# Attention: the second projection of a tile is issued behind the weighing product

## The chip, the cores and the metric

The kernel runs on one core of a Trainium2 chip. The metric is the device time of one execution in microseconds; the figure of merit is the median of repeated runs. Five engines of the core work side by side, each on its own list of instructions in order: TensorE (PE) multiplies matrices and transposes, ScalarE (ACT) applies functions and copies, VectorE (DVE) and GpSimd (POOL) work elementwise, SyncE (SP) issues transfers. They wait for each other through semaphores. In the profile PEld stands for the weight loads of TensorE.

## The reference, cut to what matters

Four layers run one after the other on a batch of four images of 64x64 pixels with 128 channels. The first three (two state-space scans and an edge-weighted mixing layer) take over nine tenths of the time and are not touched. The change lies in the fourth, neighbourhood attention with four heads of 32 channels, where each pixel looks at a 7x7 window around itself:

```python
qkv = (x @ qkv_w + qkv_b).reshape(B, H, W, 3, HEADS, HEAD_DIM)
q = qkv[..., 0, :, :] * HEAD_DIM ** (-0.5)
kk = qkv[..., 1, :, :]
v = qkv[..., 2, :, :]
...
scores = jnp.einsum('bxyhd,bxyklhd->bxyhkl', q, kwin) + bias[None]
attn = jax.nn.softmax(scores.reshape(B, H, W, HEADS, k * k), axis=-1)
...
out = jnp.einsum('bxyhkl,bxyklhd->bxyhd', attn, vwin).reshape(B, H, W, C)
return out @ proj_w + proj_b
...
gate = jax.nn.sigmoid(jax.nn.relu(x @ g1_w + g1_b) @ g2_w + g2_b)
return attn_out * gate + x
```

## The kernel before, in words

The class `Attention` (from L1964) works on tiles of 128 queries, that is two image rows; 32 tiles make an image (`NQ`), 128 tiles the batch. For a tile the keys are eight image rows, that is 512 pixels or one matmul of 512 columns for each head; a bias with a large negative number outside the 7x7 window does the masking. One tile passes through these steps, each a small method:

- `scores` (L2102, PE): four heads, 128x512 scores into a PSUM tile of four banks, `sps`, of which there is one.
- `biased` (L2113, DVE), one call for each head: adds the bias, negates and takes the minimum.
- `exponential` (L2126, ACT), one call for each head, with the row sum.
- `turn` (L2134, PE), one call for each head: four 128x128 transposes into a PSUM bank of the tag `tps`; `keep` (L2141) copies the bank to SBUF, heads 0 and 1 on ACT, heads 2 and 3 on DVE.
- `one_over` (L2155 on DVE, L2157 on POOL): the reciprocal of the row sums, spread to 128 columns.
- `weigh` (L2151, PE): the weighing product, values times turned weights, all heads, into one quarter of the PSUM tile `d`.
- `turn_others` (L2162, L2163, PE): transposes of the reciprocals and of x, into two other quarters of `d`; `inverse` (L2167, ACT) copies the first of them out.
- `divide` (L2171, DVE), then `mix` (L2174, PE: the output projection), then `result` (L2180, L2181, DVE) and the store of the result by SP (L2184).

The steps of several tiles are interleaved: a pass of the loop in `run` over `n` issues the scores of tile n, turns tile n-1, weighs tile n-2 and finishes tile n-3. The order of the calls in the loop is the order of each engine's list; the layer runs under a manual schedule, so nothing rearranges it.

Into the same loop go the projections. `project(b, c)` returns small functions, the pieces, for one chunk c of 512 pixels (four tiles), two chunks ahead of its use (`LEAD`):

- query and key: one fp32 matmul of 512 columns (L2045, L2051) and an ACT instruction that adds the bias (L2047, L2052);
- hidden: the same with 64 outputs (L2056, L2058);
- values: four matmuls of 128 columns (L2075) and one ACT copy (L2080);
- gates: four matmuls of one column (L2063), one ACT instruction (L2067) and two short DVE instructions (L2068, L2069).

A chunk has these five pieces, and the chunks 0 and 7 of an image a second values piece at the end. They are dealt to the four passes of a group:

```python
left = 4 - n % 4
now, pieces = pieces[: -(-len(pieces) // left)], pieces[-(-len(pieces) // left) :]
```

Five pieces thus fall as query+key, hidden, values, gates; six as query+key, hidden+values, gates, values. Below, a pass is called by its pieces: the query-key pass, the hidden pass and so on. Thirty chunks are projected inside the loop (two before it), so there are 30 query-key passes, and of these chunks seven have six pieces and so a hidden-values pass too: 37 passes with two pieces.

Every turn and every piece takes one bank of the tag `tps`, and there are two of them. A turn or a piece can therefore start only when the bank taken two steps earlier has been read out: by the copy of `keep`, or by the ACT instruction of the piece. In a query-key pass the banks are taken in the order turn of head 3 (tile n-2), query, key, turns of heads 0, 1, 2 (tile n-1).

Of the kernel before, what the change touches and what calls it, by code (L numbers as in the profile page):

```python
# [1870 lines left out]
def layer2(tc, C, nb, x_in, x_out, d_w, d_rel, d_v, beside, side):  # L1871
    with ExitStack() as es, tc.manual_schedule():
# [12 lines left out]
        if True:  # L1885
            with tc.tile_pool(name="last", bufs=1) as pool:
                E.pool = pool
                last = Last(tc, C, pool, E.psum, side, nb - 1, x_in)
                last.early()
                run(statistics(0, range(NCH)))  # L1890
                last.late()
                E.roots([E.rstd])
                for _ in in_turn([last.first(c) for c in range(NCH)]):
                    pass
                pieces = project(0, range(4))
                for _ in in_turn([last.second(c) for c in range(NCH)]):
                    for _ in range(2):
                        if pieces:
                            pieces.pop(0)()
                run(pieces)  # L1900
# [31 lines left out]
            gates, gather = E.gates(out, last[2], [third[2]["var"]], []), E.gather(*last, alone=True)  # L1932
            pieces = E.finish(*third)
            run(gates[:1] + rest[:2] + gates[1:2] + rest[2:4] + gates[2:4] + rest[4:] + pieces[:4] + gates[4:6])
            run(pieces[4:] + gather[:3] + E.outputs(*second) + gather[3:])
            E.roots([second[2]["var"]])
# [27 lines left out]
class Attention:  # L1964
# [221 lines left out]
    def run(self):  # L2186

        nc, total = self.nc, self.nb * NQ

        def do(f, n, *args):  # L2190
            if 0 <= n < total:
                f(n, *args)

        def chunk_of(m):
            return divmod(m, NCH)

        for m in range(self.LEAD):
            for piece in self.project(*chunk_of(m)):
                piece()
            self.load(*chunk_of(m + 2))  # L2200
            if m == 0:
                for i in range(3):
                    self.bring_bias(i)
        pieces = []
        for n in range(total + 4):
            if n % 4 == 0 and n < total:
                assert not pieces
                m = n // 4 + self.LEAD
                self.load(*chunk_of(m + 2))
                if m < self.nb * NCH:  # L2210
                    pieces = self.project(*chunk_of(m))
                if n in (4, 8):
                    self.bring_bias(2 + n // 4)
            left = 4 - n % 4
            now, pieces = pieces[: -(-len(pieces) // left)], pieces[-(-len(pieces) // left) :]
            do(self.scores, n)
            do(self.turn, n - 2, 3)
            do(self.biased, n, 0)
            do(self.biased, n, 1)
            do(self.one_over, n - 1)  # L2220
            do(self.keep, n - 2, 3, nc.vector.tensor_copy)
            do(self.exponential, n, 0)
            do(self.exponential, n, 1)
            for piece in now:
                piece()
            do(self.biased, n, 2)
            do(self.biased, n, 3)
            do(self.mix, n - 3)
            do(self.turn, n - 1, 0)
            do(self.turn, n - 1, 1)  # L2230
            do(self.keep, n - 1, 0, nc.scalar.copy)
            do(self.exponential, n, 2)
            do(self.keep, n - 1, 1, nc.scalar.copy)
            do(self.result, n - 3)
            do(self.weigh, n - 2)
            do(self.turn_others, n - 2)
            do(self.exponential, n, 3)
            do(self.inverse, n - 2)
            do(self.divide, n - 2)
            do(self.turn, n - 1, 2)  # L2240
            do(self.keep, n - 1, 2, nc.vector.tensor_copy)
# [211 lines left out]
```

## Time and profile before

| | |
|---|---|
| median of three runs | 13013.98 us (13012.62 to 13024.42) |
| the profiled execution's own time | 13014.66 us |
| its span, first to last instruction | 13012.9 us |
| busy share of the span | DVE 90%, POOL 74%, PE 72%, ACT 60% |
| scores of tile 0, of tile 127 | at 12140.0 us, at 12995.5 us of the span |

The shares are means over four layers. The attention lies in the last 870 us, and only its own part of the profile bears on the change. Times in the rows below are microseconds from the span's start; "x4" counts instructions merged into a row; what stands in brackets at the end of a row is the time that the engine stood idle before it, and the instruction that ended this. The ends of PE's rows are modelled, the starts are recorded.

### The profile page before, as it was taken

Reading aid. Unit: us, or ns where it says so; the run is one execution under the profiler, and the core shown is the slowest. Engines: PE = TensorE matmul, PEld = TensorE weight load, DVE = VectorE, ACT = ScalarE, POOL = GpSimd, SP = SyncE. Lnnn points to the kernel's source line nnn. Section 1 sums busy time; section 2 is a strip of 40 time slices with the busy share of each in tenths; the row PEclk is TensorE's granted clock in tenths of the full one; section 3 lists DMA queues with packets and bytes.
Section 4 is the critical chain, followed back from the end, with each engine's and each line's share of the span. In section 5 each row is a group of like instructions: output and inputs, shape, how many; then the busy total and the mean of one; then the engine's idle time right before and its main releaser. Section 6 shows DMA issues by size and latency. Waiting matters only on the chain.

```text
span 13012.9 us, 128062 instructions
## 1 busy us (share of the span) xinstructions
PE 9421.2 (72%) x40881; PEld 2750.7 (21%) x41435; DVE 11773.1 (90%) x7219; ACT 7773.2 (60%) x10392; POOL 9663.5 (74%) x3167
## 2 busy tenths in 40 slices
PE   6777677677777767777777677777777776765799
PEld 1111111111111111111111111112111121211455
DVE  8999999999999889999999899999999998587566
ACT  4666566665666556655666565555555554575576
POOL 6887888887878778887888788888888887165200
PEclk8888999889988888988988898888899898987899
DMA  6888888898888978898878887777887776144300
GB/s 181 211 226 229 221 221 218 216 232 216 211 224 206 219 196 212 219 227 215 211 215 214 225 209 195 206 202 198 216 202 197 199 202 175 52 121 122 72 21 18
DMA packets 873450, 2463.66 MB, mean 189 GB/s; under 512 B 141888, under 2 KB 163528, under 8 KB 865096
## 3 DMA queue, kind: packets, MB, share of 16 engines
q1 hardware_dynamic: 872775, 2455.44, 73.5%
q8 instruction: 330, 5.41, 0.2%
q14 instruction: 345, 2.82, 0.1%
HBM read 2035.79 MB, written 268.17 MB: 177 GB/s over the span
## 4 chain that ended last, share of the span: by engine, by line
DVE 34%; issue 18%; PE 15%; DMA 15%; POOL 9%; ACT 8%; SPq 2%; DVEq 0%; another core or an unknown queue 0%; POOLq 0%; ACTq 0%
DVE h L478 18%; DVE h L459 12%; DMA h<-dud 7%; POOL h L459 5%; PE ms L102 3%; PE da L467 2%; POOL delta L102 2%; ACT da L469 2%; PE yps L559 1%; ACT s L2126 1%; DMA repC<-xdd 1%; POOL low L102 1%; DVE s L2113 1%; PE B L504 1%; DMA pad<-xid 1%
## 5 line engine op out<-in xcount | busy, mean ns | idle before, releaser
L459 POOL TENSOR_TENSOR h<-h,repC 128x2048 f32<-128x2048 f32 x1536 | 6956.0, 4534 | 1488.1 <-ACT state L496 1196.8
L478 DVE TENSOR_TENSOR_SCAN h<-da,state,h 128x1024 f32<-128x1024 f32 x2304 | 5294.1, 2338 | 277.7 <-ACT da L469 164.7
L469 ACT ACTIVATE da<-da,av 128x1024 f32<-128x1024 f32 x3072 | 3327.7, 1087 | 2895.3 <-PE da L467 2463.6
L467 PE MATMUL da<-dp,spread 128*128 128x512 bf16 x5802 | 2007.3, 426 | 2409.5 <-DVE h L478 2373.2
L459 DVE TENSOR_TENSOR h<-h,B 128x2048 f32<-128x2048 f32 x1536 | 3476.8, 2264 | 184.0 <-issue 78.9
L559 PE MATMUL yps<-h,gather 128*32 128x512 f32 x12288 | 1878.5, 687 | 18.0 <-issue 5.9
L478 DVE TENSOR_TENSOR_SCAN h<-da,h 128x1024 f32<-128x1024 f32 x768 | 1719.6, 2278 | 73.7 <-ACT da L469 35.2
L467 PEld LDWEIGHTS <-spread 128*128 128x128 bf16 x6144 | 589.9, 102 | 4479.2 <-issue 4091.8
L565 PE MATMUL yps<-ones,nothing 128*128 128x512 bf16 x4197 | 1243.6, 406 | 38.5 <-issue 34.9
L102 ACT ACT_TABLE_LOAD x580 | 744.1, 1283 | 12.6 <-DMA x<-in_x_dram 2.4
L102 ACT CAST parts<-delta 128x1024 bf16<-128x1024 f32 x384 | 400.7, 1043 | 565.0 <-POOL delta L102 539.1
L565 PEld LDWEIGHTS <-nothing 128*128 128x128 bf16 x4409 | 384.9, 101 | 1234.2 <-issue 945.4
L102 POOL TENSOR_TENSOR delta<-delta,low 128x1024 f32<-128x1024 f32 x192 | 452.0, 2354 | 258.0 <-ACT low L102 206.6
L2157 POOL COPY wide_total<-total 128x128 f32<-128x128 f32 x128 | 37.8, 296 | 780.6 <-DVE total L2155 214.3
L102 PE MATMUL ms<-d,wts 128*128 128x512 f32 (+3 forms) x832 | 481.9, 691 | 165.1 <-POOL d L102 59.8
L102 PE MATMUL ms<-xd,xpdt 64*128 64x512 f32 x768 | 481.9, 710 | 105.3 <-ACT xd L102 24.5
L102 POOL TENSOR_TENSOR low<-delta,xc 128x1024 f32<-128x1024 f32 x192 | 502.9, 2619 | 9.1
L2126 ACT ACTIVATE s<-s,least 128x512 f32<-128x512 f32 x512 | 368.5, 720 | 230.1 <-DVE least L2113 224.5
L542 PE MATMUL yps<-y,ident 128*128 128x512 f32 x576 | 497.4, 953 | 4.4 <-issue 1.3
L102 ACT ACTIVATE low<-ms,av 128x512 f32<-128x512 f32 x384 | 263.9, 687 | 291.1 <-PE ms L102 264.9
L1792 POOL TENSOR_TENSOR acc<-acc,part 128x1024 f32<-128x1024 f32 x120 | 303.8, 2535 | 174.7 <-DVE part L1786 174.7
L102 POOL TENSOR_TENSOR parts<-delta,parts 128x1024 bf16<-128x1024 f32 x192 | 409.6, 2134 | 31.8 <-ACT parts L102 28.8
(295 smaller groups left out, 11071.5 us busy)
## 6 DMA issues: line engine op xcount, KB each, us to landing
h<-dud SPq DMA_DIRECT2D x3072, 512.0 KB
dp<-parts SPq DMA_DIRECT2D x2304, 64.0 KB
repC<-xdd SPq DMA_DIRECT2D x192, 512.0 KB
dud<-low SPq DMA_DIRECT2D x192, 512.0 KB
spread<-gd SPq DMA_DIRECT2D x72, 1024.0 KB
pad<-xid SPq DMA_DIRECT2D x176, 256.0 KB
x<-x SPq DMA_DIRECT2D x104, 256.0 KB
yd<-y SPq DMA_DIRECT2D x96, 256.0 KB
```

What stands on the lines that cost most here:

```text
L102: return call(*args, **kw)
L459: engine.tensor_mul(pair, pair, t.prepared[step][name].unsqueeze(1).to_broadcast([P, 2, TS]))
L467: self.nc.tensor.matmul(da[:, cols], self.C.spread[:, jj, :], dp[:, j, cols], start=True, stop=True)
L469: self.nc.scalar.activation(da, da, AF.Exp, scale=t.W.a[:, at : at + 1])
L478: nc.vector.tensor_tensor_scan(h[:, way], da[:, way], h[:, way], 0.0 if step % NSTEP == 0 else t.states[step - 1][:, u % NG : u % NG + 1], ...
L504: self.nc.tensor.matmul(rep[:, self.half(i)], t.W.pick[at, :], t.prepared[step]["xd"][at, :], start=True, stop=True)
L542: self.nc.tensor.matmul(self.like_part(yps, k), self.C.ident, self.part(t.y, k, c, b), start=True, stop=False)
L559: self.nc.tensor.matmul(out, self.C.gather[jj], rhs, start=False, stop=jj == 3)
L565: self.nc.tensor.matmul(self.live["yps"], self.C.nothing, self.C.ones16, start=False, stop=False, skip_group_check=True)
L1792: (nc.vector if alone and pair else nc.gpsimd).tensor_add(acc, acc, part)
L2113: self.nc.vector.tensor_tensor_reduce(out=self.live["s", n][:, h, :], in0=self.live["sps", n][:, h, :], in1=self.bias[case][:, h, :], scal ...
L2126: self.nc.scalar.activation(s, s, AF.Exp, scale=-1.0, bias=self.live["least", n][:, h : h + 1], accum_out=self.live["total", n][:, h : h + 1],
```

## The change

In each pass, only the first of the pass's pieces stays at its place, ahead of the last two `biased`. The second, where there is one, is issued after `weigh(n - 2)` and ahead of `turn_others(n - 2)`. In a query-key pass this moves the key, in a hidden-values pass the values. On PE the piece passes from ahead of `mix`, two turns and the weighing product to behind them; on ACT from ahead of `keep` of head 0, `exponential` of head 2 and `keep` of head 1 to behind them, still ahead of `exponential` of head 3 and `inverse`. The banks are then taken in the order turn of head 3, first piece, turn 0, turn 1, second piece, turn 2. Instructions and data stay the same.

```diff
             do(self.exponential, n, 0)
             do(self.exponential, n, 1)
-            for piece in now:
+            for piece in now[:1]:
                 piece()
             do(self.biased, n, 2)
             do(self.biased, n, 3)
...
             do(self.keep, n - 1, 1, nc.scalar.copy)
             do(self.result, n - 3)
             do(self.weigh, n - 2)
+            for piece in now[1:]:
+                piece()
             do(self.turn_others, n - 2)
             do(self.exponential, n, 3)
             do(self.inverse, n - 2)
```

## The prediction

> **What bounds the kernel now.** I read first the slices of the page, to find the attention and its clock. The last slices are it:
>
> ```profile
> PE   6777677677777767777777677777777776765799
> ...
> PEclk8888999889988888988988898888899898987899
> ```
>
> PE is busy at nine tenths there, at a nearly full granted clock: TensorE sets the pace, but is not without gaps. Next I read busy times by stretches, one for each pass of a regular group of four (core, then PE, PEld, DVE, ACT, POOL, clock, DMA):
>
> ```profile
> 12437.64:12445.54 7.90, 7.02 (x65) 3.96 (x64) 4.63 (x14) 5.95 (x16) 0.30 (x1) 1.00 0.17 52
> 12445.54:12452.09 6.55, 6.20 (x63) 3.50 (x62) 4.63 (x14) 4.76 (x14) 0.30 (x1) 1.00 0.04 10
> 12452.09:12458.54 6.45, 5.91 (x70) 4.18 (x69) 4.63 (x14) 4.52 (x13) 0.30 (x1) 1.00 0.05 12
> 12458.54:12464.66 6.12, 6.00 (x69) 4.27 (x68) 4.96 (x16) 3.85 (x12) 0.30 (x1) 1.00 0.00 0
> ```
>
> They are the query-key, hidden, values and gates pass. The query-key pass takes 7.90 us and PE works 7.02 of them; DVE and ACT have room. The clock is 1.00 in all four. Then the chain of waits inside the query-key pass:
>
> ```profile
> 12438.70 0.60 DVE st L2141
> ...
> 12440.60 0.59 DVE st L2141
> ...
> 12441.24 1.14 PE tps L2051 x2
> ...
> 12442.40 0.70 ACT k L2052
> ...
> 12443.14 0.66 PE tps L2134 x4
> 12443.80 1.01 PE d L2151 x32
> ...
> 12445.61 1.11 PE sps L2102 x8
> ...
> 12446.75 0.60 DVE s L2113
> ```
>
> The key waits for a PSUM bank until DVE has copied a turned head out (L2141), then a turn waits for the key's ACT instruction (L2052), then weighing and the next scores follow without a gap. The timeline gives the sizes:
>
> ```profile
> 12438.41 0.29 DVE L2171 TENSOR_TENSOR o<-d,inv 128x128 f32<-128x128 f32 x1 [1.02 <-ACT inv L2167]
> ...
> 12439.21 0.68 DVE L2113 CUSTOM_DVE_ANT_0 s<-sps,bias 128x512 f32<-128x512 f32 x1
> ...
> 12441.24 1.12 PE L2051 MATMUL tps<-x,w 128*128 128x512 f32 x2 [0.76 <-DVE st L2141]
> 12441.42 0.67 ACT L2047 ACTIVATE q<-tps,qb 128x512 f32<-128x512 f32 x1
> ...
> 12444.74 0.33 PE L2162 MATMUL d<-ident,wide_total 128*128 128x128 f32 x1
> 12444.77 0.73 ACT L2126 ACTIVATE s<-s,least 128x512 f32<-128x512 f32 x1
> 12445.49 0.26 ACT L2167 COPY inv<-d 128x128 f32<-128x128 f32 x1
> 12445.78 0.29 DVE L2171 TENSOR_TENSOR o<-d,inv 128x128 f32<-128x128 f32 x1 [2.49 <-ACT inv L2167]
> ```
>
> PE stands 0.76 us before the key. The last two rows matter as much: `divide` (L2171) waits for `inverse` (L2167), the last ACT instruction of a pass, and DVE is strictly behind it: the copy of head 2, then the first `biased` of the new pass. In the first two rows that `biased` starts 0.80 us after `divide`, straight behind the copy; at 12446.75 it starts 0.97 after, since it had to wait for the scores.
>
> **The change part by part.** I count from 12437.64, the query-key pass's first weight load. Nothing is added or removed; the key is moved: two weight loads and two matmuls on PE, one ACT instruction. It issues no DMA and nothing on DVE, POOL or SP; the store of `result` and the copy of `one_over` keep their places.
>
> *What it leaves.* Ahead of the key's old place nothing alters. `mix` and the first turn come next; that turn now takes the bank the key had and waits for the same copy, to 3.60. The second turn takes the query's bank: free when the query's ACT instruction ends, 12441.42 + 0.67 = 12442.09, or 4.45; a turn that waited for the key started 0.05 after its end (12442.40 + 0.70 to 12443.14), so it starts at 4.50 instead of 5.50. Gain: 1.00 us at the weighing product, which then starts at 5.16 (turn to weighing 0.66 in the chain).
>
> *What it pays on PE.* From weighing to the next scores is 1.81 us (12443.80 to 12445.61), gapless. The key goes into this stretch. Its price is the one unknown of this step: the hidden matmul, the same 512 columns in two instructions, is followed by `mix` 1.00 us after its start (12447.20 to 12448.20 in the timeline), the key of before by `mix` after 0.96. The Trainium skill, "TensorE: Matmul & The Clock Gate", section Back-to-back issue gap, gives about 216 ns for a warm matmul of 512 columns, and "FP8 and Floating Point Precision" counts four passes for true fp32: an estimate of 0.86. I take 1.00, the row, being the same instruction in the same list. Then the next scores start at 5.16 + 1.81 + 1.00 = 7.97 of the chain's scale, where they were at 12445.61, which is 7.97 too: the gap of 0.76 and the wait of the turn (0.36 by its weight load) are refilled by 1.00 of key. On PE alone the query-key pass gains 0.00 by the row and 0.14 by the rule.
>
> *What it pays on ACT.* The key's matmul starts behind the weighing product: `turn_others` starts 0.94 after weighing (12443.80 to 12444.74), so the key starts at 5.16 + 0.94 = 6.10, and its ACT instruction, as before, 1.16 later (12441.24 to 12442.40): 7.26. ACT has had nothing to do since about 6.1, where the copy of head 1 ends, but `exponential` of head 3 and `inverse` are queued behind the key. Before, they started at 7.13 and 7.85. Now the exponential starts after the key's 0.70. How much of it two neighbours overlap is shown by hidden's instruction: 0.67 long, its follower starts after 0.57. The row nearest by name, key to copy of head 0, has 0.71, but that copy came 0.75 to 0.80 after its turn's start in all four passes, so PE held it. The skill's "ScalarE: Activation LUTs", section What ACT_TABLE_LOAD costs, has ≈ 280 ns + 0.833 ns for each of 512 elements, less 93 of overlap: an estimate of 0.61. I take 0.60, from the row (0.70 less 0.10); between 0.57 and 0.71 it makes no more than 0.1. Exponential at 7.86, `inverse` 0.72 later (12444.77 to 12445.49) at 8.58, `divide` 0.29 later at 8.87, first `biased` 0.80 later at 9.67. Before: 12446.75, or 9.11.
>
> So the first `biased` of the hidden pass comes 0.56 us late although its scores are in time. What hangs on it there is all of it: exponentials, hidden's ACT instruction, the turn that waits for its bank, weighing, scores. That a late `biased` is paid in full is in the trace: query-key passes whose first `biased` came 1.57 us after their start took 7.90, those (behind a values pass) with 1.21 took 7.55: 0.35 for 0.36. In the hidden pass no second piece stands, so its tail keeps its shape and the 0.56 neither grows nor shrinks later. The banks cost nothing: the key's bank is free at about 5.0 and needed at 6.10; the next turn needs it at about 9.0, the key has left it at 7.96.
>
> *The hidden-values passes.* Counted from the first `biased`, 12500.80 in one of them: weighing comes 3.60 later (as in the hidden pass, 12446.75 to 12450.35), then values 0.94, to its copy 1.20 (12502.83 to 12504.03), copy 0.59 less 0.10, then 0.72, 0.29 and 0.80: 8.04, against 7.48 before (to 12508.28). Again 0.56, now paid in the gates pass.
>
> *Sum.* 37 passes have two pieces. The first, tile 0, has no turns and no weighing around it, and the passes behind it wait for the bias tables; I count it at 0. 36 x 0.56 = 20.2 us. The profiled execution took 14.66 past 13000, so 13034.9; the median of the runs shown is 0.7 lower, so 13034, slower by 0.15%. A measurement of this kernel can tell about 0.2%, or 26 us, from no change: the likeliest outcome lies inside it.
>
> **The rivals.**
>
> *The moved piece fills a hole and nothing is late* (faster, or none). If `divide` did not follow ACT's tail, PE alone would count: 0.00 to -0.14 for a pass, 36 x -0.14 = -5, so 13009 to 13014. For it: PE is the busiest engine and both its waits shrink. Against it: DVE's rows show 2.49 us of waiting for exactly that ACT instruction. A gain over 26 us would need 0.72 from each place: nearly all of the 1.12 waited there, with no price for the key. PE has no gap behind the weighing product where it could hide.
>
> *The key's weights are not loaded under the weighing product* (slower than 0.2%). The weighing product's loads are 32 columns wide; should the key's two loads (0.19 each) wait for its end, the first one's 0.19 comes ahead of the matmul and of everything behind it, and should ACT's overlap go as well (0.71 in place of 0.60), a place costs 0.56 + 0.19 + 0.11 = 0.86: 36 x 0.86 = 31 us, 13045. It decides from 0.72 a place. For it: the trace shows no key behind a weighing product. Against it: `turn_others`, also 128 columns wide, starts 0.94 after weighing, with 0.20 of its weight load's idle time inside that.
>
> *It does not do what it says*: the loop's order is the engines' order here, and banks are free in time, so a second piece does move. I give this nothing.
>
> **How the numbers follow.** The first case, with its terms uncertain by about 0.15 a place: 75%, from 13029 to 13040, a tenth of it over 13040 (the bound of 0.2%). The slow rival 15%. The hole filled without lateness 10%, of which 3 in 100 of all are beyond -26 us. So slower 0.15 + 0.08 = 0.23, faster 0.03, same 0.74. Range 13022 to 13045.
>
> **What would show it.** Right: query-key passes still 7.9 us; before the key PE no longer waits for L2141, instead ACT waits for the key (L2052 behind L2051) about 1.1 us where it was 0.3; the first `biased` of a hidden pass about 1.8 us after its scores start instead of 1.21; hidden passes near 7.1 instead of 6.55; values and gates passes of regular groups unchanged. The reading is wrong if hidden passes stay at 6.55, if query-key passes move by more than 0.15, or if a wait appears at the turn of head 3 for the key's ACT instruction.

## The result, and the profile after

The changed kernel took 13027.85 us (median of 20 runs) against 13010.81 us for the kernel before (20 runs): a ratio of 1.0018, 95% interval 1.0012 to 1.0025. (The means, 13030.1 and 13007.2, give this ratio; the medians are 17.0 us, or 0.13%, apart.) It is slower, inside the band of 0.2% that the prediction called likeliest, and on the side it named. The median lies 1 us below the stretch of 13029 to 13040 that the prediction's first case gave; the kernel before itself came out 3 us lower in these 20 runs than the 13014 from which the prediction counted.

The runs scatter by some 20 us either way, and much of this lies in the three unchanged layers: the profiled executions of all the kernels below reach the first scores of the attention anywhere between 12110 and 12148 us. So from here on the attention is measured by itself, from the first scores to the first `biased` of the last tile, in each kernel's trace. It took 856.7 us before and 876.8 after: 20.05 more, where the prediction's sum said 20.2. That they agree so closely is in part luck, since 1.2 of the 20.05 come from a short fall of the clock (see the last section). The profiled execution after took 13042.58 us, 27.9 over that before; the other 7.9 lie ahead of the attention.

The four passes after, by stretches (the columns are those of the view before):

```profile
12451.98:12459.79 7.81, 7.02 (x66) 4.08 (x65) 4.54 (x14) 5.04 (x13) 0.29 (x1) 1.00 0.18 52
12459.79:12466.95 7.16, 6.27 (x63) 3.51 (x63) 4.54 (x14) 5.54 (x16) 0.29 (x1) 1.00 0.03 9
12466.95:12473.40 6.45, 5.91 (x70) 4.19 (x69) 4.64 (x14) 4.53 (x13) 0.29 (x1) 1.00 0.05 12
12473.40:12479.52 6.12, 6.00 (x69) 4.27 (x68) 4.96 (x16) 3.85 (x12) 0.29 (x1) 1.00 0.00 1
```

The query-key pass is 0.09 shorter (7.81 against 7.90); the hidden pass behind it, in which nothing was moved, is 0.61 longer (7.16 against 6.55); the other two are as they were. The timeline of the query-key pass, first the key's reading before, then rows of the pass after, shows both halves:

```profile
12442.40 0.69 ACT L2052 ACTIVATE k<-tps,v 128x512 f32<-128x512 f32 x1 [0.31 <-PE tps L2051]
```

```profile
12455.57 0.66 PE L2134 MATMUL tps<-ident,s 128*128 128x128 f32 x4 [0.54 <-DVE st L2141]
...
12456.48 0.66 PE L2134 MATMUL tps<-ident,s 128*128 128x128 f32 x4 [0.25 <-ACT q L2047]
...
12458.08 1.13 PE L2051 MATMUL tps<-x,w 128*128 128x512 f32 x2
...
12459.24 0.69 ACT L2052 ACTIVATE k<-tps,v 128x512 f32<-128x512 f32 x1 [1.15 <-PE tps L2051]
...
12459.83 0.71 ACT L2126 ACTIVATE s<-s,least 128x512 f32<-128x512 f32 x1
...
12460.53 0.25 ACT L2167 COPY inv<-d 128x128 f32<-128x128 f32 x1
12460.81 0.29 DVE L2171 TENSOR_TENSOR o<-d,inv 128x128 f32<-128x128 f32 x1 [3.50 <-ACT inv L2167]
...
12461.62 0.68 DVE L2113 CUSTOM_DVE_ANT_0 s<-sps,bias 128x512 f32<-128x512 f32 x1
```

The first two rows of the pass after are the gain. The second turn waits for the query alone, and weighing comes a microsecond earlier. The key's row has no wait left: its bank is free and PE goes straight into it from the weighing product. The rest is the bill. ACT stands 1.15 us for the key (0.31 before), the exponential of head 3 and `inverse` are behind it, and DVE waits 3.50 us for `inverse` where it waited 2.49. The first `biased` of the next pass starts 1.83 us after that pass's first weight load instead of 1.21.

The chain of waits says the same by what it no longer contains. Between the key and the next `biased` it now runs over ACT and DVE:

```profile
12457.14 1.01 PE d L2151 x32
12458.15 1.07 PE tps L2051 x2
...
12459.24 0.23 ACT k L2052
...
12459.83 0.80 ACT s L2126 x2
12460.63 0.16 ACT inv L2167
...
12460.81 0.29 DVE o L2171
```

Before, the path went from weighing through the transposes to the next scores, all on PE. The next scores have left the path: they are 0.09 earlier and wait for nobody, and nobody waits for them.

### The profile page after: what moved, and what is told of

Its sections match the earlier page's. It is cut to its first block, busy times and chain, and to the rows that moved or that the text cites. A ratio compares the mean times of both kernels' runs of the same rounds, so it can differ in the third digit from the quotient of the medians.

```text
span 13040.8 us, 128062 instructions
## 1 busy us (share of the span) xinstructions
PE 9439.7 (72%) x40881; PEld 2758.4 (21%) x41435; DVE 11771.3 (90%) x7219; ACT 7764.0 (60%) x10392; POOL 9659.0 (74%) x3167
## 4 chain that ended last, share of the span: by engine, by line
DVE 36%; issue 18%; DMA 14%; PE 14%; ACT 8%; POOL 8%; SPq 1%; DVEq 0%; another core or an unknown queue 0%; POOLq 0%; ACTq 0%
DVE h L478 19%; DVE h L459 13%; DMA h<-dud 8%; POOL h L459 4%; PE ms L102 3%; PE da L467 2%; ACT s L2126 2%; POOL delta L102 2%; DMA repC<-xdd 1%; PE yps L559 1%; ACT da L469 1%; DMA pad<-xid 1%; PE B L504 1%; POOL low L102 1%; ACT hid L1686 1%
```

## Experiments

Two theories. The one of the prediction: what is paid is the lateness of ACT's tail (exponential of head 3 and `inverse` behind the key), handed on through `divide` to the next pass. The rival: what is paid is PE's time for the piece, now on the gapless stretch behind the weighing product. All lengths are of the attention, as defined above, from one traced execution each; the query-key, hidden, values and gates passes of regular groups agree within 0.02 us in nearly every place of a trace. The whole kernel was timed repeatedly only for the first (20 runs) and the seventh (12) of these edits.

**The second piece behind `inverse`.** PE has the piece behind `turn_others`, still ahead of the last turn; on ACT the tail goes first.

```diff
             do(self.weigh, n - 2)
-            for piece in now[1:]:
-                piece()
             do(self.turn_others, n - 2)
             do(self.exponential, n, 3)
             do(self.inverse, n - 2)
+            for piece in now[1:]:
+                piece()
             do(self.divide, n - 2)
```

> The second piece goes three calls further: behind inverse, so that exponential of head 3 and inverse are ahead of it on ScalarE; on TensorE it stands behind turn_others. Measured is the attention alone, from the first scores to the last tile's first biased: 856.7 us before, 876.8 us after. Theory (the lateness is ScalarE's tail queued behind the key): the first biased of a hidden pass is back at 1.21 us after its scores, hidden passes at 6.55, query-key passes stay at 7.81; attention about 854, the whole near 13011. Rival (the second piece's TensorE time behind the weighing product is what is paid): still about 877, the whole near 13034.

Measured: 854.5 us. Hidden passes 6.55, their first `biased` at 1.21 again; query-key passes 7.76. The first `biased` of a hidden pass waits for its scores again:

```profile
12427.92 0.26 ACT L2167 COPY inv<-d 128x128 f32<-128x128 f32 x1
...
12428.63 0.69 ACT L2052 ACTIVATE k<-tps,v 128x512 f32<-128x512 f32 x1 [0.45 <-PE tps L2051]
...
12430.17 0.69 DVE L2113 CUSTOM_DVE_ANT_0 s<-sps,bias 128x512 f32<-128x512 f32 x1 [0.41 <-PE sps L2102]
```

The whole against the kernel before: ratio 0.9996, interval 0.9989 to 1.0003, so no difference that can be measured, as 2.2 us would be. The rival falls: the piece's matmuls are still on the stretch behind the weighing product, and the 20 us are gone.

**PE's list exactly as in the change, ACT's alone reordered.** The last run moved the piece on PE as well, past two transposes. Here only the instruction that reads the bank is moved behind `inverse`: the pieces key and values return it as a function (that part of the edit is left out).

```diff
...
-            for piece in now[1:]:
-                piece()
+            reads = [piece() for piece in now[1:]]
             do(self.turn_others, n - 2)
             do(self.exponential, n, 3)
             do(self.inverse, n - 2)
+            for read in reads:
+                read()
```

> TensorE's list is left as in the changed kernel, second piece directly behind the weighing product; only the ScalarE instruction that reads its bank goes behind exponential of head 3 and inverse. Theory (ScalarE's order is the cause): inverse follows turn_others at about 7.2 instead of 8.55, hidden passes start their first biased at 1.21, attention about 854. Rival (TensorE's place is the cause): 877, since TensorE's list is the same as after.

Measured: 854.5 us, with query-key passes at 7.81, as in the change, and hidden passes at 6.55. The timeline (DVE's `biased` is the first of the hidden pass):

```profile
12437.64 0.27 ACT L2175 COPY inv<-d 128x128 f32<-128x128 f32 x1 [0.71 <-PE d L2171]
12437.80 0.69 ACT L2054 ACTIVATE k<-tps,v 128x512 f32<-128x512 f32 x1
...
12439.12 0.69 DVE L2121 CUSTOM_DVE_ANT_0 s<-sps,bias 128x512 f32<-128x512 f32 x1 [0.30 <-PE sps L2110]
```

`inverse` now waits for PE's transposes, not for the key, and the `biased` waits 0.30 for its scores again. With PE's list the same, the order of three ACT instructions is worth 22 us, or 21 without the fall of the clock in the change's trace.

**The key's reading doubled.** The dose: the instruction ahead of ACT's tail is issued twice.

```diff
-            nc.scalar.activation(im["k"][:, cols], ps, AF.Identity, bias=self.kb)
+            for _ in range(2):
+                nc.scalar.activation(im["k"][:, cols], ps, AF.Identity, bias=self.kb)
```

> As the changed kernel, but ScalarE reads the key's bank twice with the same result, so the instruction ahead of exponential of head 3 is doubled. Theory (every bit of lateness of ScalarE's tail is paid in the next pass): the first biased of hidden passes at 1.83 + 0.59 = 2.42, 29 places x 0.59 = 17 us more, attention about 894. Rival (TensorE's place): unchanged at 877.

Measured: 896.2 us, 19.4 over the change; first `biased` of hidden passes at 2.56, hidden passes 7.89 where they were 7.16. Query-key passes stay at 7.81, since PE does not notice. The first `biased` moves by 0.73 and the pass by 0.73: paid in full, as the theory has it (29 x 0.73 = 21). The 29 places do add 21.0 between them, and the first group gives back 1.4. A gates pass stretched by a fall of the clock is in both traces (8.21 and 8.17 us) and drops out of the difference. The dose itself was larger than the expected 0.59:

```profile
12454.35 1.41 ACT L2053 ACTIVATE k<-tps,v 128x512 f32<-128x512 f32 x2 [1.14 <-PE tps L2051]
...
12455.66 0.71 ACT L2127 ACTIVATE s<-s,least 128x512 f32<-128x512 f32 x1
```

Two readings take 1.41 between them, and the exponential starts 1.31 after the first, not 2 x 0.59. The second reading writes the same place as the first and does not overlap with it; that it is the shared output that forbids the overlap was not tried.

**The key read by VectorE.** Place and lateness of the key are those of the change; another engine reads the bank.

```diff
-            nc.scalar.activation(im["k"][:, cols], ps, AF.Identity, bias=self.kb)
+            nc.vector.tensor_scalar_add(im["k"][:, cols], ps, self.kb)
```

> As the changed kernel, but the key's bank is read by VectorE (a tensor_scalar with the bias), which idles there for inverse, in place of ScalarE. Theory: exponential of head 3 starts at about 6.0 instead of 7.85, divide follows the key's reading at about 7.9, the first biased of hidden passes is bound by the scores again (1.21); only the seven hidden-values passes still pay 0.55 each: attention about 858. Rival (the key comes late, whoever reads it, or TensorE's place): 877.

Measured: 858.9 us, hidden passes 6.55 with their `biased` at 1.21. In gates passes behind hidden-values passes, where the values are still read by ACT, it stays at 1.74, as in the change.

```profile
12416.51 0.75 DVE L2052 TENSOR_SCALAR k<-tps,v 128x512 f32<-128x512 f32 x1 [1.92 <-PE tps L2051]
...
12416.78 0.27 ACT L2167 COPY inv<-d 128x128 f32<-128x128 f32 x1 [0.71 <-PE d L2163]
...
12417.17 0.28 DVE L2171 TENSOR_TENSOR o<-d,inv 128x128 f32<-128x128 f32 x1
12417.37 0.68 DVE L2141 COPY st<-tps 128x512 f32<-128x512 f32 x1
...
12418.26 0.69 DVE L2113 CUSTOM_DVE_ANT_0 s<-sps,bias 128x512 f32<-128x512 f32 x1 [0.21 <-PE sps L2102]
```

The reading is as late as in the change, ahead of `divide` even, but it lies in DVE's idle time beside ACT's tail instead of ahead of it: `inverse` no longer waits for it, and the last row waits 0.21 for the scores. It is not the late key that costs, but what is queued behind its reading on ACT.

**The second piece directly ahead of the weighing product.**

```diff
+            for piece in now[1:]:
+                piece()
             do(self.weigh, n - 2)
-            for piece in now[1:]:
-                piece()
             do(self.turn_others, n - 2)
```

> The second piece one call earlier than in the change: directly ahead of the weighing product. Theory (only ScalarE's tail counts): the key's ScalarE instruction starts at about 6.3 instead of 7.26, exponential of head 3 at 6.9, inverse at 7.6, first biased possible at 8.7 and so bound by the scores at 9.0; hidden passes at 6.55; attention about 854.5, as with the piece behind inverse. Rival (a piece between the turns and turn_others lengthens TensorE's path): 877.

Measured: 855.8 us, hidden passes at 6.55, query-key passes at 7.85. One call earlier than in the change is enough to give ACT's tail its room.

With the cause settled, what is there to gain? The other wait in the timeline of the change is the second turn's for the first piece's reading: 0.25 in its row, 0.49 by its weight load. That reading stands on ACT behind two exponentials, and its matmul has been done for some time.

**The first piece ahead of the exponential of head 1**, on the kernel before:

```diff
             do(self.exponential, n, 0)
-            do(self.exponential, n, 1)
-            for piece in now:
+            for piece in now[:1]:
                 piece()
+            do(self.exponential, n, 1)
+            for piece in now[1:]:
+                piece()
```

> The kernel before, but the first piece is issued ahead of exponential of head 1 instead of behind it; the second piece stays behind it, as before. The second turn waits for the first piece's ScalarE instruction in hidden and values passes (0.49 and 0.38 us by its weight load). Theory: that instruction comes 0.7 us earlier and TensorE gains about 0.3 in a hidden pass and 0.2 in a values pass (then ScalarE's tail binds); the query-key pass, whose second turn waits for the key, gains nothing. Attention about 856.7 - 29 x 0.5 = 842. Rival (the turn is bound by its first copy or by the exponentials, which are now later): 857 or more.

Measured: 844.7 us. Hidden passes 6.34 (6.55), values passes 6.35 (6.45), gates passes 6.03 (6.12); query-key passes do not gain (7.92), since their second turn waits for the key. Hidden-values passes lose 0.26 (7.74 against 7.48), which was not expected: in them the values' matmul now waits for hidden's reading, where before it waited for the copy of head 3, so the bank behind the first piece is another one than before. It is the same in the query-key passes, and in the next two kernels: the taker directly behind the query waits for the query's reading. Why the two banks change places is not shown.

**Both: first piece early, second piece behind `inverse`**:

```diff
             do(self.exponential, n, 0)
-            do(self.exponential, n, 1)
             for piece in now[:1]:
                 piece()
+            do(self.exponential, n, 1)
```

(besides the first experiment's edit)

> Both: first piece ahead of exponential of head 1, second piece behind inverse. Theory: the query-key pass gains as well, since its second turn waits for the query alone: another 0.3; with 0.3, 0.2 and the 0.1 already seen about 0.9 a group, attention about 854.5 - 29 x 0.8 = 831, the whole about 0.2% faster than before. Rival (DVE or ScalarE's tail binds at once): 845 to 854, no measurable difference.

Measured: 825.9 us, and 12975.77 us for the whole: ratio to the kernel before 0.9975, interval 0.9967 to 0.9984. It is faster than both kernels. By stretches:

```profile
12420.75:12428.06 7.31, 6.57 (x65) 4.05 (x64) 4.82 (x15) 5.59 (x16) 0.29 (x1) 1.00 0.18 56
12428.06:12434.41 6.35, 6.00 (x64) 3.53 (x63) 4.45 (x14) 4.61 (x11) 0.29 (x1) 1.00 0.04 10
12434.41:12440.76 6.35, 5.75 (x71) 4.23 (x70) 4.54 (x14) 4.64 (x13) 0.29 (x1) 1.00 0.05 13
12440.76:12446.79 6.03, 5.96 (x70) 4.30 (x70) 4.77 (x16) 4.31 (x13) 0.29 (x1) 1.00 0.00 0
```

The group takes 26.04 us against 27.02 before. The query-key pass gains most, 0.59: once freed from the key, the turns wait only for the query's reading, which is early, and the second follows the first without a wait (x8 in the row are two turns):

```profile
12424.36 1.09 PE L2134 MATMUL tps<-ident,s 128*128 128x128 f32 x8 [0.74 <-ACT q L2047]
```

In this pass, moving the key alone gains 0.14 and moving the first piece alone nothing; they stood in series on the same turn.

**First piece early, second piece ahead of the weighing product**:

```diff
+            for piece in now[1:]:
+                piece()
             do(self.weigh, n - 2)
```

(in place of behind `inverse`)

> First piece ahead of exponential of head 1, second piece directly ahead of the weighing product. Theory: as with the second piece behind inverse if ScalarE's tail has room: attention about 831; if the tail is now the bound (TensorE's passes have become 0.3 shorter), the key in ScalarE's tail is paid in part: up to 29 x 0.3 = 9 us more, 840.

Measured: 846.4 us, worse than the 831 to 840 expected, and for another reason than the tail:

```profile
12430.05 0.30 PEld L2051 LDWEIGHTS tps<-x,w 128*128 128x128 f32 x2 [0.53 <-ACT st L2141]
```

The key takes the bank of the first turn, and this must be copied out by ACT first (`keep` of head 0). With the turns earlier, PE reaches the key before that copy is done and stands there, with the weighing product behind it. Hidden passes are fine (6.34); query-key passes take 7.87 instead of 7.31. Of these 0.56, the wait makes 0.36 (key 1.39 after the start of the turns, where the weighing product of the kernel above comes 1.03 after it). The rest is the key's price on PE, which depends on its neighbours: 1.05 from its start to the weighing product here, 0.86 more from weighing to the next scores there. The tail was in time, and the bank was not.

## Why the prediction was right, point by point

Times from the query-key pass's first weight load, 12451.98 after:

| step | predicted | measured |
|---|---|---|
| second turn | 4.50 | 4.50 |
| key's matmul | 6.10 | 6.10 |
| key's reading on ACT | 7.26 | 7.26 |
| exponential of head 3 | 7.86 | 7.85 |
| `inverse` | 8.58 | 8.55 |
| `divide` | 8.87 | 8.83 |
| first `biased` of the next pass | 9.67 | 9.64 |
| the next pass's first weight load | 7.90 | 7.81 |

- *The price of a place.* 0.56 predicted, 0.53 measured between the first `biased` of the two passes, in 27 of the 29 groups behind the first (0.42 in the other two); about the same (0.48 to 0.55) in the pass from hidden-values to gates.
- *The key on PE.* Taken at 1.00 from the hidden matmul's row; measured, weighing to the next scores grew from 1.82 to 2.73, so 0.91: nearer to the prediction's estimate of 0.86 (from the Trainium skill, "TensorE: Matmul & The Clock Gate", section Back-to-back issue gap, and "FP8 and Floating Point Precision", section TensorE Precision Notes) than to the row that was chosen. (That section calls its 216 ns the gap of an isolated matmul and has 131 for a stream of them; the estimate of 0.52 that this would make is borne out by no row here.) It changed nothing of the sum, since the scores are not what the next `biased` waits for.
- *The reading's step on ACT.* 0.60 chosen; measured 0.59 (12459.24 to 12459.83). The 0.71 of the row nearest by name was rightly put aside as held by PE.
- *The hidden pass.* Said to be near 7.1: 7.16, counted from its first weight load, because that comes 0.09 earlier.
- *What was missed is small.* The first group, counted at nothing, paid 0.3. One gates pass took 8.21 us where its like took 6.65: in the trace the granted clock falls there (last section), and with the 0.35 that the next pass gave back it adds some 1.2 us to the 20.05. The other 18.8 are the 36 places at 0.42 to 0.55 each, the first group's 0.3, and hundredths elsewhere.
- *The rival of the weight loads* asked for a place above 0.72; the key's loads show 0.20 of idle time ahead of them and its matmul starts as early as `turn_others` did. Its mechanism did not occur.
- *A reading in the rivals was off.* The 0.72 that a gain over 26 us would need from each place is two thirds of the 1.12 waited there, not nearly all. Nothing else rests on it.
- *The rival of the filled hole* fell as argued: DVE waited 1.01 us longer for `inverse` than before.

## What to carry to other kernels

When an instruction is moved into a gap of the busiest engine, follow its result to the engine that reads it, and see what is queued behind that reading: here PE gained 0.09 a pass and ACT's order handed 0.62 to the next one. Where two waits are in series on one step (the second turn waited for the key, and behind that for the query), removing either alone shows almost nothing, and removing both gives more than the sum. A bank that rotates among several users is a second order beside the lists: with the key's place in it unchanged, making the turns earlier made the key wait.

## What the runs showed of the hardware

Two ACT instructions that write the same 128x512 place one after the other were 0.72 us apart, while the same reading with another instruction behind it freed the engine after 0.59. The granted clock, 1.00 all through the attention's regular passes, fell there for a moment in two of the ten traces: to 0.50 for 3.4 us in that of the change, from 12750.51, and as much in that with the key's reading doubled, from 12295.15. In each it stretched one pass by about a quarter (8.21 us and 8.17 against 6.65). In the change's trace PE had been busy for 4.43 of the 5 us before the row in which the clock falls (0.66 is the mean of that row's 5 us); what brought it about is not shown.

```profile
12745.00:12750.00 5.00, 4.43 (x35) 3.06 (x33) 2.77 (x8) 2.71 (x7) 0.29 (x1) 1.00 0.00 0
12750.00:12755.00 5.00, 5.00 (x54) 3.69 (x54) 2.65 (x10) 3.26 (x10) 0.00 (x0) 0.66 0.06 16
```
